# A four-block graph network on one core: a comparison of edge types goes to GpSimd, four bias rows are loaded at two places, and the last output tile is added and stored in halves

## The chip, the core and the metric

The kernel runs on one core of a Trainium2 chip. The core has five engines that run their own queues of instructions and wait for each other by semaphores: TensorE (PE, matrix products into PSUM), VectorE (DVE), ScalarE (ACT), GpSimd (POOL) and SyncE (SP), which here only issues transfers. Transfers between the chip's memory (HBM) and the on-chip SBUF are issued from SP, from GpSimd and, twice at the start, from ScalarE, and are carried out by 16 DMA engines. The metric is device microseconds of one execution; lower is better.

## The reference

A graph has 1024 nodes with 512 features each (x) and 17408 edges (src, dst, sorted by dst), the loops among them. Each edge has 4 attributes for block 1, 8 for its small network, a type of 8 and a weight. Four blocks follow each other, each of the form x + block(relu(layernorm(x))):

```
block 0: adj (deduplicated, symmetric, with loops), scaled by 1/sqrt(degree) on both sides; adj @ (h @ W) + bias
block 1: w = network(edge attributes 8) -> 4 x 128 per edge; messages w * up(h)[src] * edge attributes 4;
         sums by dst; a linear map out
block 2: twice  h @ W0 + (norm-weighted sum of h over edges) @ W1 + b;  between them
         layernorm * gamma + beta and a leaky relu   (rows b1, gamma, beta, b2 of 512)
block 3: twice  h @ loop + bias + sum over 4 bases of (sums by dst of coef * h[src]) @ basis,
         coef = comp[type of the edge] * weight of the edge; a relu between them
```

The output is x after block 3, 1024x512 in float32.

## The kernel before, in words

Nodes lie in 8 tiles of 128. Edges lie in 136 tiles of 128, taken two at a time as 68 groups. Because edges are sorted by destination, the two tiles of a group fall in a window of 32 nodes; the kernel checks that at run time and has a general path for other graphs (`stack(False)`), which isn't taken here.

*Counting (about 30 to 97 us).* A matrix `cnt` of 1024x1024 counts the edges between nodes. For each group VectorE has made one-hot rows by comparing a ramp with the edge's source (`ro`, 128x1024) and its destination in the window (`co`, 128x2048), for eight edge tiles at a time (`places`, L504); TensorE multiplies them into PSUM (`pc`, L532), and VectorE adds the product into the window of `cnt` (L545). Between these, TensorE does the rest of block 0's dense layer (`pz`, L251) and the first 13 of 17 batches of the edge network (`hidden`: `pm` on TensorE, L453, an activation on ScalarE, L455, and a write of the third layer to the table `hidtab` in HBM, L458, from SP for batches 0, 3, 6 and 9 and from GpSimd for the others). TensorE's order in this stage is fixed as written. The load of the edge types (`relations`, L434, 64 rows of 2176) is issued from SP behind the write of batch 6; `related` (L440) compares them with the row's own number and is written in the code at group 59 of 68 (`if g == NG * 7 // 8`). Its result feeds 34 small products (`related_bases`, `pr`, L594), which come after the products `pa` (L618, L620) that turn the finished counts into adjacency.

*Block 1 (about 165 to 476 us).* Per group, TensorE makes the edge weights (`pw`, L819) from a batch of `hidtab` rows that SP has fetched (`fetch`, L576; two buffers, a new batch every four groups, listed in `fetched`); GpSimd gathers the source rows of two tiles (L290) and weights the window (`yo`, L859); ScalarE and VectorE make the messages (L836 to L841); TensorE sums them (`pg`, L885) and VectorE adds the sums (L888). Among these, block 2's weights are loaded, and GpSimd subtracts blocks of them (`sums_of_blocks`, L765).

*Block 2 (about 476 to 690 us).* The rows b1, gamma, beta and b2 are spread to 128 partitions by four loads from SP (`bias_row`, L104; four buffers in rotation, shared with the bias of block 0 and those of block 3). b1 is added at L986, gamma and beta used at L1008 and L1009, and b2 added at L1011. The code stands behind block 1's, but the four loads are tied behind one fetch:

```
with tc.issue_after(fetched[8]):
    b1 = bias_row("L2_gnn_b1", f"b1{fast}")
    gamma = bias_row("L2_gnn_gamma", f"gamma{fast}")
    beta = bias_row("L2_gnn_beta", f"beta{fast}")
    b2 = bias_row("L2_gnn_b2", f"b2{fast}")
```

*Block 3 (about 690 to 1219 us).* Twice over 68 groups: gathers (L290), a weighted window (`wo`, L1135), sums `ps` (L1149) and their addition (L1168). As soon as a node tile has all its edges, its products with the four bases follow (`products`, `po`, 16 per tile, L1094); `ready` adds the result, and in the second layer stores the tile (L1086, L1087). The last tiles' products stand at the end.

*What sets the order.* A planner goes over the traced instructions and puts each in the queue of its engine, using its own estimate of when its inputs are there; instructions further down in the code may come earlier in a queue. `tc.issue_after(ins)` keeps what is traced under it, on the engine of `ins`, behind `ins`. `pinned` keeps the instructions of the named engines in the order in which they are written. Otherwise only data and buffers hold an instruction back.

Of the kernel before, what the change touches and what calls it, by code (L numbers as in the profile page):

```python
# [15 lines left out]
ALU = mybir.AluOpType  # L16
# [5 lines left out]
P = 128  # L22
N = 1024
NB = N // P
D = 512
KC = D // P
# [5 lines left out]
NREL = 8  # L32
NBAS = 4
# [16 lines left out]
def gnn_stack(ctx, tc, a, out, xtab, htabs, hidtab):  # L50
# [6 lines left out]
    nc = tc.nc  # L57
# [25 lines left out]
    x = const.tile([P, NB, D], F32, name="x")  # L83
# [74 lines left out]
    r8 = const.tile([P, 1], F32, name="r8")  # L158
# [120 lines left out]
    def split(terms, n, z, scale, name, rest=None):  # L279

        hi, mid, lo = (t[:, n, :] for t in terms)
        nc.scalar.activation(hi, z, AF.Copy, scale=scale)
        if rest is None:
            rest = work.tile([P, D], F32, tag="h", name=f"rest_{name}", bufs=4)
        nc.vector.scalar_tensor_tensor(rest, z, scale, hi, op0=ALU.mult, op1=ALU.subtract)
        nc.scalar.copy(mid, rest)
        return nc.vector.tensor_sub(lo, rest, mid).ins
# [59 lines left out]
    with pinned(PE):  # L347
# [7 lines left out]
        for _ in first:  # L355
# [8 lines left out]
                                            op0=ALU.add, op1=ALU.subtract))  # L364
# [22 lines left out]
    def stack(fast):  # L387
# [43 lines left out]
        def relations(pool):  # L431

            types = pool.tile([8 * NREL, E // 8], I32, name="types")
            nc.sync.dma_start(types, bass.AP(tensor=a["edge_type_8"].tensor, offset=0, ap=[[E // 8, 8], [0, 8], [1, E // 8]]))  # L434
            return types

        def related(types):

            rel = types.bitcast(F32)
            nc.vector.tensor_scalar(rel, types, r8[: 8 * NREL], None, op0=ALU.is_equal)  # L440
            return rel


# [33 lines left out]
        with tc.tile_pool(name=f"ohs{fast}", bufs=6 if fast else 4) as ohs, pinned(PE):  # L477
            if fast:
# [44 lines left out]
                for g in range(NG):  # L523
# [11 lines left out]
                    if behind and behind[0] in written:  # L535

                        with tc.issue_after(written[behind[0]]):
                            if behind.pop(0) == 6:
                                types = relations(rels)
                            else:  # L540
                                next(loads)
                    if g == NG * 7 // 8:
                        rel = related(types)
                    part = cnt[:, :, bass.ds(base(g), W)]
                    nc.vector.tensor_add(part, part, pc.rearrange("p (i w) -> p i w", w=W))  # L545
            else:
# [6 lines left out]
                for g in range(ET // B):  # L553
# [3 lines left out]
                    for i in range(NB):  # L557
                        for j in range(2):
                            ps = bank(f"pc_{g}_{i}_{j}")
                            for k in range(B):  # L560
                                nc.tensor.matmul(ps, so[k][:, i * P : (i + 1) * P], do[k][:, j * 512 : (j + 1) * 512],
                                                 start=(k == 0), stop=(k == B - 1))
# [9 lines left out]
        hq, fetched = {}, []  # L572
# [38 lines left out]
        if fast:  # L611

            degs = small.tile([P, 2, NB], F32, tag="degs", name="degs", bufs=1)
            for i in range(NB):
                for j in range(2):
# [3 lines left out]
                    for q in range(4):  # L619
                        nc.tensor.matmul(pt[:, q * P : (q + 1) * P], cnt[:, 4 * j + q, i * P : (i + 1) * P], ident16,  # L620
                                         start=False, stop=(q == 3))
# [36 lines left out]
        for n in range(NB):  # L658
            if fast:
                last = split(terms, n, zs0[:, n, :], dinv[:, n : n + 1], f"0_{n}")  # L660
# [148 lines left out]
        with tc.tile_pool(name=f"l1e{fast}", bufs=2 if fast else 1, reuse_waits="tile") as l1e:  # L809
# [43 lines left out]
            if fast:  # L853
# [16 lines left out]
                for g in range(NG):  # L870
# [11 lines left out]
                    for i in range(len(prods[0])):  # L882
                        for k in range(G):
                            lhsT, rhs, b, n = prods[k][i]
# [32 lines left out]
        with tc.tile_pool(name=f"l2{fast}", bufs=1) as l2:  # L917
# [3 lines left out]
            else:  # L921
                terms1 = [l2.tile([P, NB, D], F32, tag="parts1", name="zs2")]
            y = stage
            with tc.issue_after(fetched[8]):
                b1 = bias_row("L2_gnn_b1", f"b1{fast}")
                gamma = bias_row("L2_gnn_gamma", f"gamma{fast}")
                beta = bias_row("L2_gnn_beta", f"beta{fast}")
                b2 = bias_row("L2_gnn_b2", f"b2{fast}")

# [98 lines left out]
            def bases(l):  # L1028

                ws = [load_w(a[f"L3_gnn_basis{l}"][b], f"basis{l}_{b}{fast}") for b in range(2)]  # L1030
                return ws + [[load_half(w_l0[h], a[f"L3_gnn_basis{l}"][2], h) for h in range(2)]]

            loops = {0: loop_weights(0)}
            w3 = [loops[0][0]] + bases(0)
# [30 lines left out]
        with tc.tile_pool(name=f"l3{fast}", bufs=1, reuse_waits="tile") as l3:  # L1065

            sums = l3.tile([P, KC, NBAS, N], F32, name="sums")
# [9 lines left out]
            def ready(l, n, po):  # L1077

                if l == 0:
                    nc.vector.tensor_add(hb[:, n, :], hb[:, n, :], po)  # L1080
                    nc.scalar.activation(hb[:, n, :], hb[:, n, :], AF.Relu)  # L1081
                    nc.sync.dma_start(htabs[1][n * P : (n + 1) * P, :], hb[:, n, :])
                    if fast:
                        nc.gpsimd.memset(sums.rearrange("p c b d -> p (c b) d")[:, :, n * P : (n + 1) * P], 0.0)
                else:
                    nc.vector.tensor_add(x[:, n, :], x[:, n, :], po)  # L1086
                    nc.sync.dma_start(out[n * P : (n + 1) * P, :], x[:, n, :])  # L1087

            def products(l, n, w3):

                po = bank2(f"po3_{l}_{n}")[:, 0, :]
                for b in range(NBAS):
                    for c in range(KC):
                        nc.tensor.matmul(po, sums[:, c, b, n * P : (n + 1) * P], chunk(w3[1 + b], c),  # L1094
                                         start=(b == 0 and c == 0), stop=(b == NBAS - 1 and c == KC - 1))
                        if b == NBAS - 1 and c == KC - 1:
                            ready(l, n, po)
                        yield

            for l in range(2):  # L1100
                if l == 1:
                    w3 = [loops[1][0]] + bases(l)
# [3 lines left out]
                with tc.tile_pool(name=f"l3e{l}{fast}", bufs=3 if fast else 1, reuse_waits="tile") as l3e:  # L1106
# [24 lines left out]
                    if fast:  # L1131
# [10 lines left out]
                        for g in range(NG):  # L1142
# [8 lines left out]
                            n = {0: 3, 1: 4, 2: 5, 4: 6, 6: 7}.get(g)  # L1151
# [19 lines left out]
                    else:  # L1171
                        for g in range(NG):
                            m = gathered(g)
                            for b in range(NBAS):
                                for j in range(2):
# [5 lines left out]
                                    for c in range(KC):  # L1181
                                        ps = bank(f"ps_{l}_{g}_{b}_{j}_{c}")
                                        for k in range(G):
                                            nc.tensor.matmul(ps, m[k][:, c * P : (c + 1) * P], wo[:, k, :],
                                                             start=(k == 0), stop=(k == G - 1))
# [75 lines left out]
```

## Time and profile before

| | us |
|---|---|
| median of three runs | 1225.16 |
| the three runs | 1224.23, 1227.38, 1225.16 |
| the profiled execution | 1221.29 |
| its span, first to last instruction | 1219.5 |
| TensorE busy in it | 1195.6 |
| VectorE busy | 661.8 |
| GpSimd busy | 580.5 |
| ScalarE busy | 295.0 |

The profile is of one execution. Its rows give an engine, a line of the kernel, what is written from what, shapes and counts; times in brackets are idle time of that engine just ahead, with what ended it. The chain that ended last is followed back from the last instruction: at each step to what released it, or to the one before it on its engine. PEld is TensorE's loading of weights, which runs beside its products. A name with q (DVEq, SPq) is an engine's own queue, where register work, waits and issues are done. "issue" is time in which an engine waited for nothing that the profile shows. The clock granted to TensorE was 0.994 of full speed over the span.

### The profile page before, as it was taken

Reading aid. Unit: us, or ns where it says so; the run is one execution under the profiler, and the core shown is the slowest. Engines: PE = TensorE matmul, PEld = TensorE weight load, DVE = VectorE, ACT = ScalarE, POOL = GpSimd, SP = SyncE. Lnnn points to the kernel's source line nnn. Section 1 sums busy time; section 2 is a strip of 40 time slices with the busy share of each in tenths; the row PEclk is TensorE's granted clock in tenths of the full one; section 3 lists DMA queues with packets and bytes.
Section 4 is the critical chain, followed back from the end, with each engine's and each line's share of the span. In section 5 each row is a group of like instructions: output and inputs, shape, how many; then the busy total and the mean of one; then the engine's idle time right before and its main releaser. Section 6 shows DMA issues by size and latency. Waiting matters only on the chain.

```text
span 1219.5 us, 17420 instructions
## 1 busy us (share of the span) xinstructions
PE 1195.6 (98%) x6322; PEld 795.8 (65%) x6322; DVE 661.8 (54%) x1244; ACT 295.0 (24%) x693; POOL 580.5 (48%) x641
## 2 busy tenths in 40 slices
PE   7999999999999999999999999999999999999998
PEld 3445557767777778644444567777776577777774
DVE  5888647786777775776774433333332153333331
ACT  4435364434444443432332400000000000000000
POOL 2011346686666663443121266566661586555540
PEclk9999999989999999999999999999999999999999
DMA  3331045545544442002002366555552666556540
GB/s 114 124 125 36 22 155 165 151 139 153 151 139 139 139 130 85 21 22 65 1 9 92 101 193 206 160 164 157 165 163 65 199 170 194 162 162 170 157 129 17
DMA packets 55166, 149.77 MB, mean 123 GB/s; under 512 B 8796, under 2 KB 10272, under 8 KB 55008
## 3 DMA queue, kind: packets, MB, share of 16 engines
q0 software_dynamic: 33360, 109.34, 31.3%
q1 hardware_dynamic: 21424, 38.71, 9.6%
q8 instruction: 52, 0.85, 0.3%
q10 hardware_dynamic: 288, 0.52, 0.1%
q14 instruction: 42, 0.34, 0.1%
HBM read 135.70 MB, written 12.85 MB: 122 GB/s over the span
## 4 chain that ended last, share of the span: by engine, by line
PE 89%; DVE 4%; issue 2%; DMA 2%; ACT 1%; POOL 1%; DVEq 0%; SPq 0%; ACTq 0%; POOLq 0%
PE ps L1149 19%; PE po L1094 18%; PE pg L885 14%; PE pu L275 10%; PE pw L819 10%; PE p L955 7%; PE pl L251 4%; PE pm L453 2%; PE po L803 1%; PE pz L251 1%; PE pt_l L241 1%; PE pc L532 1%; DVE cnt L545 1%; PE pup L689 1%; DMA w_mlp<-in_L_gnn_W_mlp_dram 1%
## 5 line engine op out<-in xcount | busy, mean ns | idle before, releaser
L290 POOL DMA_INDIRECT m<-htab_dram,src_i x272 | 261.2, 960 | 165.6 <-PE ps L1149 116.9
L1149 PEld LDWEIGHTS ps<-wo,m 128*128 128x128 f32 x2176 | 261.6, 192 | 57.3 <-issue 56.0
L1149 PE MATMUL ps<-wo,m 128*128 128x128 f32 x2176 | 262.2, 275 | 0.7 <-DMA m<-htab_dram,src_i 0.7
L885 PEld LDWEIGHTS pg<-yo,msg 128*128 128x128 f32 x1632 | 194.6, 193 | 35.9 <-issue 17.8
L885 PE MATMUL pg<-yo,msg 128*128 128x32 f32 (+1 forms) x1632 | 189.8, 274 | 2.7 <-DVE msg L841 1.5
L1168 DVE TENSOR_TENSOR sums<-sums,ps 128x512 f32 x136 | 93.7, 689 | 156.7 <-PE po L1094 133.8
L836 ACT ACTIVATE dot<-s,ea 128x128 f32<-128x128 f32 x408 | 130.0, 390 | 165.7 <-DVE msg L841 107.5
L290 POOL DMA_INDIRECT s<-xtab_dram,src_i x136 | 132.8, 976 | 36.4 <-issue 24.5
L819 PE MATMUL pw<-w_mlp,hq 128*128 128x512 f32 x272 | 135.1, 620 | 0.0
L1135 DVE TENSOR_TENSOR wo<-ohw,cwTrue 128x256 f32<-128x256 f16 x136 | 65.9, 487 | 103.5 <-PE ps L1149 103.5
L859 POOL TENSOR_TENSOR yo<-ohw,ea 128x160 f32<-128x160 f16 x136 | 63.1, 486 | 66.6 <-PE pg L885 66.5
L275 PE MATMUL pu<-parts,cnt 128*128 128x512 bf16 x384 | 84.8, 379 | 0.0
L837 DVE TENSOR_TENSOR msg<-pw,s 128x512 f32<-128x512 f32 x68 | 47.0, 692 | 47.3 <-PE pw L819 35.6
L819 PEld LDWEIGHTS pw<-w_mlp,hq 128*128 128x128 f32 x272 | 47.2, 193 | 34.0 <-issue 34.0
L275 PEld LDWEIGHTS <-cnt 128*128 128x128 f16 x384 | 37.6, 98 | 44.9 <-issue 2.3
L838 DVE TENSOR_TENSOR msg<-s,pw 128x768 f32<-128x768 f32 x68 | 64.2, 944 | 0.0
L1094 PE MATMUL po<-basis_0True,sums 128*128 128x512 f32 x128 | 60.8, 600 | 0.4
L1094 PE MATMUL po<-basis_3True,sums 128*128 128x512 f32 x128 | 59.8, 594 | 0.8 <-DVE sums L1168 0.8
L1081 ACT ACTIVATE stage<-stage 128x512 f32<-128x512 f32 x8 | 5.0, 630 | 226.9 <-DVE stage L1080 226.9
L1094 PE MATMUL po<-w_l,sums 128*128 128x512 f32 x128 | 59.9, 593 | 0.0
L1094 PE MATMUL po<-basis_1True,sums 128*128 128x512 f32 x128 | 59.9, 593 | 0.0
L888 DVE TENSOR_TENSOR acc<-acc,pg 128x256 f32 x68 | 28.7, 422 | 46.7 <-PE pg L885 46.7
(208 smaller groups left out, 1355.2 us busy)
## 6 DMA issues: line engine op xcount, KB each, us to landing
hq<-hidtab_dram SPq DMA_DIRECT2D x17, 256.0 KB, 2.9
m<-htab_dram,src_i POOLq DMA_INDIRECT x272, 3.6
hidtab_dram<-hid POOLq DMA_DIRECT2D x9, 256.0 KB, 2.3
s<-xtab_dram,src_i POOLq DMA_INDIRECT x136, 3.6
xtab_dram<-up SPq DMA_DIRECT2D x8, 256.0 KB, 2.0
b_1True<-in_L_gnn_W_dram SPq DMA_DIRECT2D x4, 512.0 KB, 5.0
w_l<-in_L_gnn_basis_dram SPq DMA_DIRECT2D x4, 512.0 KB, 4.3
basis_0True<-in_L_gnn_basis_dram SPq DMA_DIRECT2D x4, 512.0 KB, 4.0
```

The source lines that it names most:

```text
L275: nc.tensor.matmul(pu, m[:, s, d * P : (d + 1) * P], z[:, s, :], start=(s == 0 and j == 0), stop=(s == NB - 1 and j == len(zs) - 1))
L290: nc.gpsimd.indirect_dma_start(out=g, out_offset=None, in_=table, in_offset=bass.IndirectOffsetOnAxis(ap=idx[:, t : t + 1], axis=0))
L819: nc.tensor.matmul(pw[:, k, :], hq[q][:, (t % 4) * P : (t % 4 + 1) * P], w_mlp4[:, t // 4 % 2, :], start=True, stop=True)
L836: nc.scalar.activation(dot[:, k, m, :], s1[:, k, m, :], AF.Copy, scale=ea[:, g * G + k, 1 + m : 2 + m])
L838: nc.vector.tensor_mul(msg[:, :, 2:5, :], s1, w[:, :, 2:3, :].to_broadcast([P, G, 3, MUL]))
L859: nc.gpsimd.tensor_mul(yo[:, k], ohw[:, t, :].unsqueeze(1).to_broadcast([P, NY, W]), ea[:, t, :].unsqueeze(2).to_broadcast([P, NY, W]))
L885: nc.tensor.matmul(ps[:, b : b + n, :], lhsT, rhs, start=(k == 0), stop=(k == G - 1))
L955: nc.tensor.matmul(p, lhs[:, c, :], rhs[:, c, :], start=(c == 0), stop=(c == 1))
L1094: nc.tensor.matmul(po, sums[:, c, b, n * P : (n + 1) * P], chunk(w3[1 + b], c), start=(b == 0 and c == 0), stop=(b == NBAS - 1 and c == KC ...
L1135: nc.vector.tensor_mul(wo, ohw[:, ts, :].unsqueeze(2).to_broadcast([P, G, NBAS, W]), cw[:, l, ts, :].unsqueeze(3).to_broadcast([P, G, NBAS ...
L1149: nc.tensor.matmul(ps[:, c * P : (c + 1) * P], m[k][:, c * P : (c + 1) * P], wo[:, k].rearrange("p b w -> p (b w)"), start=(k == 0), stop= ...
L1168: nc.vector.tensor_add(part, part, ps.rearrange("p (i w) -> p i w", w=W))
```

## The change

Three edits. `related` runs on GpSimd in place of VectorE, with the same operands. The rows b1 and gamma are tied behind `fetched[9]`, and beta and b2 behind `fetched[12]`. In the second layer of block 3, node tile 7 is added and stored in two halves of 256 columns; the other tiles are as before. (A local name `last` in `products` only shortens its text.)

```
-            nc.vector.tensor_scalar(rel, types, r8[: 8 * NREL], None, op0=ALU.is_equal)
+            nc.gpsimd.tensor_scalar(rel, types, r8[: 8 * NREL], None, op0=ALU.is_equal)
...
-            with tc.issue_after(fetched[8]):
+            with tc.issue_after(fetched[9]):
                 b1 = bias_row("L2_gnn_b1", f"b1{fast}")
                 gamma = bias_row("L2_gnn_gamma", f"gamma{fast}")
+            with tc.issue_after(fetched[12]):
                 beta = bias_row("L2_gnn_beta", f"beta{fast}")
                 b2 = bias_row("L2_gnn_b2", f"b2{fast}")
...
-                    nc.vector.tensor_add(x[:, n, :], x[:, n, :], po)
-                    nc.sync.dma_start(out[n * P : (n + 1) * P, :], x[:, n, :])
+                    for h in (slice(0, D // 2), slice(D // 2, D)) if n == NB - 1 else (slice(0, D),):
+                        nc.vector.tensor_add(x[:, n, h], x[:, n, h], po[:, h])
+                        nc.sync.dma_start(out[n * P : (n + 1) * P, h], x[:, n, h])
```

More of the change, by code (lines that the diff above doesn't have):

```diff
@@ L1093, in products @@
                     for c in range(KC):
-                        nc.tensor.matmul(po, sums[:, c, b, n * P : (n + 1) * P], chunk(w3[1 + b], c),
-                                         start=(b == 0 and c == 0), stop=(b == NBAS - 1 and c == KC - 1))
-                        if b == NBAS - 1 and c == KC - 1:
+                        last = b == NBAS - 1 and c == KC - 1
+                        nc.tensor.matmul(po, sums[:, c, b, n * P : (n + 1) * P], chunk(w3[1 + b], c), start=(b == 0 and c == 0), stop=last)
+                        if last:
                             ready(l, n, po)
```

## The prediction

> **What bounds the kernel now.** I read the page first (busy shares), then the chain that ended last, once for the whole span and once around each of the three places that the change touches, and then the instructions there in order of time. The page's shares:
>
> ```profile
> PE 1195.6 (98%) x6322; PEld 795.8 (65%) x6322; DVE 661.8 (54%) x1244; ACT 295.0 (24%) x693; POOL 580.5 (48%) x641
> PE 89%; DVE 4%; issue 2%; DMA 2%; ACT 1%; POOL 1%; DVEq 0%; SPq 0%; ACTq 0%; POOLq 0%
> ```
>
> TensorE is 98% busy and carries 89% of the chain, so an edit elsewhere pays only where the chain leaves TensorE. Does it at the three places? First the counting: the chain between 74 and 92 us.
>
> ```profile
> 74.61 0.43 DVE cnt L545
> 75.08 0.39 PE pc L532 x2
> 75.47 0.86 PE pm L453 x2
> ...
> 78.86 0.42 DVE cnt L545
> 79.32 0.39 PE pc L532 x2
> ...
> 81.69 0.61 ACT hid L455
> ...
> 87.00 0.99 PE pz L251 x2
> 87.99 0.23 PE pc L532 x2
> 88.22 0.86 PE pz L251 x2
> ```
>
> Up to about 80 us the chain keeps passing through VectorE (the count's additions, and behind "issue" its one-hot comparisons); from 81 us it is TensorE and ScalarE alone. Now VectorE itself around the comparison that moves:
>
> ```profile
> 87.84 1.34 DVE L440 TENSOR_SCALAR types<-types,r 64x2176 f32<-64x2176 int32 x1
> 89.11 0.41 DVE L545 TENSOR_TENSOR cnt<-cnt,pc 128x256 f32 x1
> ...
> 94.75 0.42 DVE L545 TENSOR_TENSOR cnt<-cnt,pc 128x256 f32 x1 [0.28 <-PE pc L532]
> 95.83 0.42 DVE L545 TENSOR_TENSOR cnt<-cnt,pc 128x256 f32 x1 [0.67 <-PE pc L532]
> ```
>
> The comparison takes 1.34 us at a time when the chain is elsewhere, and the last additions wait for TensorE (0.28 and 0.67 us): VectorE has caught up. Second, the chain where the four bias rows are issued (300.1 to 302.0 us):
>
> ```profile
> 299.72 2.60 PE pg L885 x24
> 302.32 1.80 PE pw L819 x4
> 304.12 2.60 PE pg L885 x24
> 306.71 1.80 PE pw L819 x4
> 308.51 2.60 PE pg L885 x24
> ```
>
> It is TensorE without a gap, one group each 4.40 us. Third, the end, in order of time:
>
> ```profile
> 1215.65 0.69 DVE L1086 TENSOR_TENSOR x<-x,po 128x512 f32<-128x512 f32 x1 [13.04 <-PE po L1094]
> 1216.37 0.33 SPq L1087 DMA_DIRECT2D out_dram<-x  x1
> ```
>
> Here all is exposed: one addition, one store, and the span's end at 1219.5 us.
>
> **The base.** The profiled execution took 1221.29 us for its span of 1219.5, 1.79 us lying around it. It is 3.87 us below the median of the three runs shown (1225.16; 1224.23 to 1227.38). I sum differences on the profiled execution and add them to the median.
>
> **Edit 1, the types compared by GpSimd.** Removed: 1.34 us of VectorE at 87.84. What it hid behind is TensorE's row of eight pz steps and nine pc pairs up to 96.65, with waits only for ScalarE's copies (0.45 and 0.67 us). Worth: 0. If that cover were gone, 1.34 us at most. Late next is TensorE itself.
>
> Added: one instruction of 64x2176 with one tensor input on GpSimd. The trace has none like it, so I bound its duration D by GpSimd's rows. The memset of 128x4096 took 3.51 us, 0.86 ns an element: D = 1.9 us. The additions of 128x512 with two inputs took 1.28 us alone, 2.5 ns an element: D = 5.4 us. The 128x128 multiplication at L141 has the instruction's own operation, took 0.73 us, and taken whole (5.7 ns an element) gives 12.4 us. But the VectorE comparison co started inside that multiplication (77.62 against 77.38) and took 1.31 us instead of 1.22, so it was held up 0.09 us, not 0.49. I take it that most of the 0.73 us was waiting, and D is nearest to the one-input memset: 2.2 us, with 1.9 and 5.4 as ends and 12.4 as the far one.
>
> When does it run? The planner puts ready GpSimd work early: the block subtractions of L765 stand in the code at groups 28 to 56 and ran from 249 to 265 us, around groups 16 to 19. So I expect the comparison not at group 59 but as soon as the types land. Their load was issued at 64.66, no landing is shown; loads of 512 KB took 4 to 6 us, so about 70 us. That is where the chain still runs over VectorE. What a GpSimd operation can do to VectorE is shown by these rows, in order of time:
>
> ```profile
> 252.84 1.28 POOL L765 TENSOR_TENSOR t_1True<-b_1True 128x512 f32<-128x512 f32 x1
> 252.91 5.98 DVE L839 TENSOR_TENSOR dot<-dot 128x256 f32<-128x256 f32 x1
> ...
> 254.06 2.50 POOL L765 TENSOR_TENSOR b_1True<-b_1True 128x512 f32<-128x512 f32 x2
> ```
>
> An addition of two SBUF tensors that takes 0.42 us elsewhere started 0.07 us after GpSimd and took 5.98 us, as long as GpSimd ran without a pause. The reverse also stands in the trace: one GpSimd addition at L667 took 5.71 instead of 1.26 us beside the 4.74 us comparison at L672. The count's additions read one operand from PSUM; the comparisons ro (0.69 us) and co (1.22 us) read two from SBUF. They come once in four groups, 1.8 of some 3.9 us; a GpSimd operation that ends within the other 2.1 us costs nothing. A start right after co (70.84 us) leaves ro at 72.88 as the next that can be held: it loses D - 2.0, 0.2 us. A start just ahead of ro loses all of D, 2.2 us. If ro or co runs first, GpSimd waits for them and is in the first case. Averaged over the moment at which the types land: 1.8/3.9 x 0.2, and 2.1/3.9 x 1.2 (the mean of 0.1 and 2.2), together +0.7 us. The ends are 0 and +5.4; a gain is excluded but for the 1.34 above.
>
> The Trainium skill, page "SBUF — State Buffer", section "Who interferes with whom", says that the pair of ports shared by the two engines is an exclusive lock, that a VectorE instruction with two SBUF inputs contends with a GpSimd one that reads SBUF, and that the second to start is blocked until the first ends. The 5.98 us row agrees, and goes further, as several GpSimd instructions were waited out. By the rule alone a GpSimd start ahead of ro costs all of D, +2.2 in place of +0.7.
>
> Queued behind the new instruction on GpSimd are the remaining writes of hidden rows (71.83, 79.66, 81.50, 86.20). If it waits for the types at 70 us and runs 2.2, the write of 71.83 goes about 0.5 us later; six hidden buffers are in rotation and the fetch of those rows comes in the next stage, so 0. Placed two writes earlier, the write of 65.88 would wait some 6.5 us and ScalarE's next use of that buffer with it: up to 4 us, a mishap of the same sign that I keep in the range. After 86.2 the next GpSimd work is at 117.46. The 34 products pr that read the result start at 104.48, so the result may be over 15 us late.
>
> **Edit 2, the bias rows.** Each is one issue on SP of 0.38 to 0.43 us and 256 KB, landing after 4.8 to 6.6 us. Two move from 300.1 behind the fetch at 317.34, two behind the one three further (each 17.6 us apart, so 370). Nothing else on SP stands between the fetches, and a fetch is issued a group ahead of its use. The buffers are free (the last user of the fourth, the first bias, ended at 131.9). First use is at 484.31 (b2) and 507.39 (b1), over 110 us later. The waits for gathers at 303 to 309 (up to 2.14 us) are ScalarE's, and TensorE goes on at 4.40 us. So: 0 removed, 0 added. With cover gone the bound is a row's landing, 6.6 us; a gain is excluded, as the chain there has no gap to close.
>
> **Edit 3, the last tile in halves.** Now: addition 0.69, issue at 1216.37, end at 1219.5. After: two additions of 128x256, each 0.42 us by L545, the second starting 0.33 after the first (such additions start at 260.27, 260.61 and 260.94), so the second ends at 1216.39, +0.05. SP issues the first store at about 1216.12; issues in a row stand 0.48 apart (300.12, 300.60, 301.07), so the second is at 1216.60, +0.23. It moves 128 KB in place of 256; between 1217 and 1218 the engines were 70% busy at 262 GB/s, so the whole took about 0.9 us and half saves 0.44. Net -0.2 us. Ends: -0.4 (no delay in issue) and +0.5 (nothing saved, an issue of 0.48 added).
>
> The Trainium skill, page "DMA: Bandwidth & Descriptors", section "Anatomy of one DMA", gives some 2.0 us fixed for each DMA (told there of those that GpSimd issues), mostly the receipt of the last byte, which halving doesn't shorten; it speaks against two stores. The trace has 2.0 us from issue to landing for 256 KB (the shortest of eight), no more than that; by the page alone nothing is saved and edit 3 is +0.2.
>
> **Sum.** 0 + 0.7 + 0 - 0.2 = +0.5 us: 1221.8 for the profiled execution, 1225.7 on the median.
>
> **The rivals.**
> *GpSimd holds VectorE for long* (slower). Place: 70 to 80 us, where the chain runs over cnt L545. For: the 5.98 us row, and L141's duration taken whole. Against: co was held only 0.09 us beside L141, and the write of 71.83 keeps GpSimd from an early block. D = 5.4 gives up to +5.2 in all, 1230.4; D = 12.4, less 2.0 of free time, gives +10.2, 1235.4. It decides by more than 3.7 us from D = 5.9 upward with a start after co, or 3.9 just ahead of ro.
> *The planner orders later work differently* (faster). The message groups' products began at 249.61, 253.84, 259.64 and 268.94; at 4.40 us each the last was due at 262.8. It was 6.1 us late, for two held additions (5.98 and 3.13 us). Another order could undo that, 1225.7 - 6.1 = 1219.6, or add as much again, 1231.8. For: GpSimd's queue is planned and an instruction is added to it. Against: the added one is 150 us earlier, the moved rows 40 us later, and neither is on that queue at that place.
> *The comparison does not move early*: it runs behind the write of 86.20, VectorE gains 1.34 us that nobody waits for, total -0.2, 1225.0.
>
> **How the numbers follow.** Forecast 0.36 and its near relative, the late comparison, 0.25; held for long 0.27, of which 0.23 beyond 3.7 us; planner 0.12, 0.08 of it faster, 0.04 slower. A difference under 0.3% (3.7 us) is about what a measurement of this kernel can tell from no change. Faster 0.08; slower 0.23 + 0.04 = 0.27; within 0.65. The likeliest's own range is 1223.5 to 1228.5 (the runs' spread of 1 to 2 us about the median, and the ends of edit 3). For 8 in 10 I leave out the faster case (0.08) and the longest D (about 0.1): 1222 (the forecast less the runs' spread and edit 3's gain) to 1232 (D = 5.4 in full with the runs' spread).
>
> **What would show it.** Right: a GpSimd row at L440 of 1.9 to 2.7 us near 70 us; ro or co near it longer by under 1 us; first pa product within 1 us of 96.49; pg still at 4.40 us from 300 to 380; two stores at the end and the span ending within 0.5 us after its last addition as now. Wrong: L440 over 5 us on GpSimd with a long ro or co inside it; hidden activations waiting for a write; or groups in the message stage in another order, which would show as a changed start of pg after 265 us.

## The result, and the profile after

| | before | after |
|---|---|---|
| median, 22 runs each (us) | 1223.65 | 1226.46 |
| lowest and highest (us) | 1218.97, 1227.38 | 1221.65, 1231.62 |
| the profiled execution, its span (us) | 1221.29, 1219.5 | 1228.83, 1227.0 |

The ratio after to before is 1.0030, 95% interval 1.0018 to 1.0043: 3.7 us slower, 2.2 to 5.3 (the means of the 22 runs lie 3.7 us apart, the medians 2.8). The time lies in the predicted range (1222 to 1232) and 0.8 us from the forecast of 1225.7. But the forecast's own difference was +0.5 us, so it is the difference that has to be explained. The two profiled executions lie 7.5 us apart, further than the medians; the runs of the kernel before fall into two groups, near 1220 and near 1226 us, and its profile is from the lower one.

The page's shares and the chain's hardly moved:

```profile
PE 1197.2 (98%) x6306; PEld 797.0 (65%) x6322; DVE 666.4 (54%) x1244; ACT 295.0 (24%) x693; POOL 587.6 (48%) x642
PE 90%; DVE 4%; issue 2%; DMA 2%; ACT 1%; POOL 1%; DVEq 0%; SPq 0%; ACTq 0%; POOLq 0%
```

GpSimd is busy 7.1 us more, VectorE 4.6 us more although the comparison has left it, TensorE 1.6 us more for the same products. Nothing here says where. The first product `pa` behind the counting does: it began at 96.49 us before, at 103.85 after, and from it to the span's end it is 1123.0 us before and 1123.15 after. All of the difference in these two executions arises ahead of it (1.3 us of the 7.4 was there at GpSimd's first write of hidden rows, 45.79 against 44.48 us, ahead of any edit). So the view to read is the counting, in order of time. GpSimd first, then VectorE, then TensorE:

```profile
67.17 0.54 POOL L458 DMA_DIRECT2D hidtab_dram<-hid  x1 [6.72 <-ACT hid L455]
73.44 5.80 POOL L440 TENSOR_SCALAR types<-types,r 64x2176 f32<-64x2176 int32 x1 [5.73 <-DMA types<-in_edge_type_dram]
79.21 0.62 POOL L458 DMA_DIRECT2D hidtab_dram<-hid  x1
```

```profile
70.14 0.68 DVE L504 TENSOR_TENSOR ro<-ramp,row 128x1024 f16<-128x1024 f16 x1
...
73.91 5.77 DVE L504 TENSOR_TENSOR ro<-ramp,row 128x1024 f16<-128x1024 f16 x1
79.61 1.30 DVE L504 TENSOR_TENSOR co<-ramp,col 128x2048 f16<-128x2048 f16 x1
```

```profile
81.29 0.59 PE L532 MATMUL pc<-co,ro 128*128 128x256 f16 x2 [5.30 <-DVE cnt L545]
81.68 1.91 PE L453 MATMUL pm<-hid,w_mlp 128*128 128x512 f32 x2
...
85.95 1.02 PE L453 MATMUL pm<-hid,w_mlp 128*128 128x512 f32 x2
```

The comparison stands between two writes of hidden rows and took 5.80 us. It began 0.47 us ahead of a `ro`, and that `ro` took 5.77 us instead of 0.68, to 0.4 us past the comparison's end. TensorE then stood 5.30 us, named as a wait for the count. When it starts again its products are slower: 1.91 us for a pair that takes 1.02 four microseconds later. The stretches show why (us, then busy time of TensorE, its weight loads, VectorE, ScalarE and GpSimd, then the granted clock, DMA share and GB/s):

```profile
76.00:78.00 2.00, 0.00 (x0) 0.00 (x0) 2.00 (x1) 0.60 (x1) 2.00 (x1) 1.00 0.97 271
78.00:80.00 2.00, 0.00 (x0) 0.10 (x1) 2.00 (x2) 0.00 (x0) 1.97 (x3) 0.66 1.00 301
80.00:82.00 2.00, 0.71 (x3) 0.64 (x3) 1.66 (x3) 0.00 (x0) 1.30 (x1) 0.50 0.77 276
82.00:84.00 2.00, 2.00 (x5) 0.61 (x5) 1.54 (x4) 0.38 (x1) 0.00 (x0) 0.50 0.07 27
84.00:86.00 2.00, 2.00 (x8) 0.96 (x6) 1.80 (x3) 0.30 (x2) 0.00 (x0) 0.63 0.00 0
86.00:88.00 2.00, 2.00 (x8) 0.83 (x8) 1.77 (x4) 1.11 (x2) 0.10 (x1) 1.00 0.00 0
```

While TensorE idles its clock falls, to 0.50 by 80 us, and it is full again from 86. The work lost to it is 0.71 x 0.50 + 2 x 0.50 + 2 x 0.37 = 2.1 us. The wait and the clock together are 7.4 us, of which some replaces waits that were there before (TensorE was idle 0.7 us between 72 and 80 in the kernel before, too). So the counting is 6.1 us longer in this pair (7.4 less 1.3), while all runs together differ by 3.7; the record has no profile of the kernel before from its upper group, and why the runs differ by less than this pair isn't shown.

The other two places. The bias rows, on SP, and the chain at the time of the first two:

```profile
325.42 0.42 SPq L104 DMA_DIRECT2D row_b1True<-in_L_gnn_b_dram  x1
325.89 0.42 SPq L104 DMA_DIRECT2D row_gammaTrue<-in_L_gnn_gamma_dram  x1
...
378.18 0.43 SPq L104 DMA_DIRECT2D row_betaTrue<-in_L_gnn_beta_dram  x1
```

```profile
320.62 2.60 PE pg L885 x24
323.22 1.80 PE pw L819 x4
325.01 2.60 PE pg L885 x24
327.61 1.80 PE pw L819 x4
```

One group still takes 4.40 us, with no gap. And the end: the last addition is now

```profile
1223.34 0.75 DVE L1088 TENSOR_TENSOR x<-x,po 128x256 f32<-128x256 f32 x2 [13.05 <-PE po L1097]
```

From its start to the span's end it is 3.66 us, where it was 3.85 before.

### The profile page after: what moved, and what is told of

Its sections match the earlier page's. It is cut to its first block, busy times and chain, and to the rows that moved or that the text cites. A ratio compares the mean times of both kernels' runs of the same rounds, so it can differ in the third digit from the quotient of the medians.

```text
span 1227.0 us, 17411 instructions
## 1 busy us (share of the span) xinstructions
PE 1197.2 (98%) x6306; PEld 797.0 (65%) x6322; DVE 666.4 (54%) x1244; ACT 295.0 (24%) x693; POOL 587.6 (48%) x642
## 4 chain that ended last, share of the span: by engine, by line
PE 90%; DVE 4%; issue 2%; DMA 2%; ACT 1%; POOL 1%; DVEq 0%; SPq 0%; ACTq 0%; POOLq 0%
PE ps L1151 19%; PE po L1097 18%; PE pg L885 14%; PE pu L275 10%; PE pw L819 10%; PE p L956 7%; PE pl L251 4%; PE pm L453 3%; PE po L803 1%; PE pz L251 1%; PE pt_l L241 1%; PE pc L532 1%; PE pup L689 1%; DMA w_mlp<-in_L_gnn_W_mlp_dram 1%; DVE cnt L545 1%
```

## The experiments

Each ratio is against the kernel before, run beside it on the same chip. The chips differ (medians of the kernel before: 1232.8 and 1236.2 us in the first two sets, 1222.6 and 1222.2 in the later ones), so only ratios are compared between sets, and from profiles of different sets only what single instructions and waits take. Diffs are against the kernel before, except where said. A small difference that shows in the profile can be lost in the median over the runs, so for the causes I read both.

**1. Which edit costs the time?** Edit 1 alone:

```
-            nc.vector.tensor_scalar(rel, types, r8[: 8 * NREL], None, op0=ALU.is_equal)
+            nc.gpsimd.tensor_scalar(rel, types, r8[: 8 * NREL], None, op0=ALU.is_equal)
```

> Edit 1 alone (types compared by GpSimd; rows and last tile as before). Theory A, GpSimd locks VectorE out: the whole loss is here, 3 to 7 us over the kernel before; the comparison takes 5.8 us near 73 us, one ro takes about as long instead of 0.68, TensorE idles some 5 us and its granted clock falls to half for some 6 us; first adjacency product pa at about 103 us, against 96.5. Theory B, the moved rows or the halved store cost it: no loss here, within 1 us of before.

Edits 2 and 3 alone:

```
-            with tc.issue_after(fetched[8]):
+            with tc.issue_after(fetched[9]):
...
+            with tc.issue_after(fetched[12]):
...
+                    for h in (slice(0, D // 2), slice(D // 2, D)) if n == NB - 1 else (slice(0, D),):
+                        nc.vector.tensor_add(x[:, n, h], x[:, n, h], po[:, h])
+                        nc.sync.dma_start(out[n * P : (n + 1) * P, h], x[:, n, h])
```

> Edits 2 and 3 without edit 1 (types compared by VectorE). Theory A: -0.2 us against before, not to be told from no change; pg at 4.40 us throughout 300 to 400 us; time from the last addition's start to the end of the span 3.66 us, against 3.85 before. Theory B: 3 to 4 us slower, with a gap in pg where the rows land (318 or 370 us).

All three, with GpSimd's comparison held back behind the last `co` by a small copy that reads it (diff against the changed kernel):

```
-                    if g == NG * 7 // 8:
-                        rel = related(types)
+                    if g == NG * 7 // 8 + 1:
+                        late = small.tile([P, 8], F32, tag="late", name="late", bufs=1)
+                        with tc.issue_after(nc.gpsimd.tensor_copy(late, nxt[1][:, 0, :8, 0]).ins):
+                            rel = related(types)
```

> All three edits, but the comparison on GpSimd is held until the last co is written (about 91 us), by a small copy of it on GpSimd. Theory A: the comparison still takes 1.9 to 5.8 us, but VectorE has only additions with a PSUM operand then; no ro or co is long, TensorE doesn't idle, pa starts within 1 us of 96.5, and the kernel is within 1 us of before. If a comparison on GpSimd were costly in any place (theory C: slower hand-over to the products pr, or code loading on GpSimd), the loss would stay at 3 us or more, or pr would start later than 8 us after the first pa.

Measured, 12 runs each. Edit 1 alone: 1.0028 (1.0008 to 1.0049). Edits 2 and 3: 1.0015 (0.9994 to 1.0035), not told apart from no change; its profile has 176.00 us of TensorE in the 176 between 300 and 476 us. All three with the comparison late: 0.9995 (0.9976 to 1.0014). The loss is edit 1's, and it goes when the same instruction runs elsewhere. It is no shorter there:

```profile
90.33 1.22 DVE L504 TENSOR_TENSOR co<-ramp,col 128x2048 f16<-128x2048 f16 x1
91.47 0.94 DVE L547 TENSOR_TENSOR cnt<-cnt,pc 128x256 f32 x2
91.62 0.19 POOL L544 CAST late<-co 128x8 f32<-128x8 f16 x1 [3.77 <-DVE co L504]
91.80 5.79 POOL L440 TENSOR_SCALAR types<-types,r 64x2176 f32<-64x2176 int32 x1
```

5.79 us, but with no `ro` or `co` left that could meet it; the additions with an operand in PSUM beside it keep their 0.42 us. The first `pa` starts at 97.61 us, 1.1 later than before, of which 0.9 was there at GpSimd's first write (45.42 us). Theory A, a lock, stands; B (the other edits) has no support, and C (the comparison costs wherever it runs) falls.

**2. What makes the comparison 5.8 us?** Four probes on GpSimd at 139 to 159 us, on the buffer of the types, which is free by then. They were added to the changed kernel, though the expectation speaks of the kernel before:

```
+                    probe = nc.gpsimd.tensor_scalar(rel, rel, r8[: 8 * NREL], None, op0=ALU.is_equal).ins
...
+                    probe = nc.gpsimd.tensor_scalar(rel, rel.bitcast(I32), r8[: 8 * NREL], None, op0=ALU.is_equal).ins
...
+                    probe = nc.gpsimd.tensor_scalar(rel, rel, 2.0, None, op0=ALU.mult).ins
...
+                    nc.gpsimd.tensor_copy(rel, rel.bitcast(I32))
```

> The kernel before, with four instructions more on GpSimd between 130 and 160 us, each on the comparison's own 64x2176 buffer, whose values are no longer used by then: the comparison with f32 read, with int32 read, a multiplication by a fixed number in f32, and a copy from int32 to f32. H (the 5.80 us come from the int32 reading): the f32 comparison takes 1.9 to 3 us and the int32 one 5.8. I (GpSimd takes 2.67 ns for each element in any one-input arithmetic): comparison 5.8 for both types, multiplication about the same, copy about the same. J (the comparison, or its operand that is a column of the tile, is the dear part): both comparisons 5.8, multiplication and copy under 3. VectorE's additions of two SBUF tiles beside them are held for as long as each runs.

The groups of that stretch (busy us, mean ns of one):

```profile
L670 POOL TENSOR_SCALAR types<-types,r 64x2176 f32<-64x2176 f32 x1 | 5.8, 5797 | 0.0
L672 POOL TENSOR_SCALAR types<-types,r 64x2176 f32<-64x2176 int32 x1 | 5.8, 5776 | 0.1
L674 POOL TENSOR_SCALAR types<-types 64x2176 f32<-64x2176 f32 x1 | 5.7, 5720 | 0.1
L676 POOL CAST types<-types 64x2176 f32<-64x2176 int32 x1 | 2.0, 1992 | 0.1
```

Neither the integers nor the comparison: arithmetic with one input takes 2.6 to 2.7 ns a column on GpSimd, a copy 0.92. The last clause of that expectation was not tested, because VectorE had no addition of two SBUF tiles there: its reductions and its operations with an operand in PSUM ran beside these probes at their own durations (1.21 and 0.74 us), as they do without them. Theory I holds for arithmetic, not for the copy.

**3. Does the loss follow the length?** Only half, or a quarter, of the columns on GpSimd early, the rest on VectorE at group 59 (diff against the changed kernel; 32 in place of 16 for the quarter):

```
-            nc.gpsimd.tensor_scalar(rel, types, r8[: 8 * NREL], None, op0=ALU.is_equal)
+            half = E // 16
+            nc.gpsimd.tensor_scalar(rel[:, :half], types[:, :half], r8[: 8 * NREL], None, op0=ALU.is_equal)
+            nc.vector.tensor_scalar(rel[:, half:], types[:, half:], r8[: 8 * NREL], None, op0=ALU.is_equal)
```

> All three parts of the change, but GpSimd compares only the first half of the columns early; the other half stays on VectorE at group 59 (0.67 us there, half of 1.34). A (the comparison locks VectorE out for as long as it runs, and the clock falls when TensorE idles over some microseconds): GpSimd's comparison takes 2.9 us (half of 5.80), ro beside it 2.5 us instead of 5.8, TensorE's wait for the count after it about 2.4 us instead of 5.3 to 5.5, and the granted clock stays near 1.00 between 78 and 86 us, where the changed kernel had 0.50; the loss is under half of the changed kernel's, 0 to 1.5 us of its 3.4. F (the loss comes from the comparison's wait for the types, 5.73 us, which stands in GpSimd's queue ahead of a write of the hidden rows): the wait is the same with half the columns, so the loss is the same, 2.8 us or more, and ratio 1.002 to 1.003. G (a fixed cost of GpSimd's first comparison): 4 us or more for half the columns, and a loss near the whole.

> As the half, with a quarter of the columns on GpSimd (1.45 us by A) and three quarters on VectorE at group 59 (1.0 us). A: ro 1.2 us instead of 5.8, the wait of TensorE behind it under 1.3 us, clock 1.00, and a time within 0.1% of the kernel before. F: the same loss as the changed kernel, 2.8 us or more. G: 4 us or more for the quarter too.

Half: 0.9995 (0.9967 to 1.0023); quarter: 0.9984 (0.9957 to 1.0011). GpSimd took 3.05 and 1.66 us, the wait for the types in front of it was the same as before (5.83 and 5.73 us), and the clock stayed at 1.00. So G falls, and F, taken as the whole cause, does too. But A had a miss of its own, in GpSimd's and VectorE's rows of the half:

```profile
73.58 3.05 POOL L441 TENSOR_SCALAR types<-types,r 64x1088 f32<-64x1088 int32 x1 [5.83 <-DMA types<-in_edge_type_dram]
```

```profile
73.97 1.31 DVE L506 TENSOR_TENSOR ro<-ramp,row 128x1024 f16<-128x1024 f16 x1
75.21 1.21 DVE L506 TENSOR_TENSOR co<-ramp,col 128x2048 f16<-128x2048 f16 x1
```

`ro` was to be held 2.5 us, to GpSimd's end at 76.63. It was out at 75.28, and `co` ran at its own length with GpSimd still at work. The lock is not held to the end. In the quarter `ro` took 0.68 us, where A expected 1.2.

**4. How long is it held?** Comparisons of several widths on GpSimd, on 64 rows beside the types, each meant to start ahead of a `ro`, by way of a small copy of `co` and a filler of 544 columns:

```
+                tried = {3: [E // 8], 6: [E // 16], 9: [E // 32] * 4, 12: [3 * E // 32], 15: [E // 16] * 2}
...
+                        for width in [E // 32] + tried[j]:
+                            with tc.issue_after(behind_co):
+                                behind_co = nc.gpsimd.tensor_scalar(tries[:, :width].bitcast(F32), tries[:, :width], r8[8 * NREL :], None, op0=ALU.is_equal).ins
```

> The kernel before, with comparisons of different widths tried on GpSimd during the counting, on 64 rows of their own beside the types: behind the 3rd, 6th, 9th, 12th and 15th column comparison (co) of VectorE comes a filler of 544 columns, and then one of 2176 columns, one of 1088, four of 544, one of 1632, and two of 1088, so placed that the next ro falls under them. L (a GpSimd comparison holds VectorE's two-operand comparisons to its end only when it is long; a short one lets them in after 0.6 us or at once, as with 1088 and 544 columns before): ro under 2176 takes 4 us or more, under 1088 1.3 us or less, under four of 544 and under two of 1088 no more than 1.5 us, and 1632 shows where the limit lies. M (any GpSimd comparison may hold or let in, by the moment at which the two meet): no order by width; ro beside 2176 may be as short as 0.7 us, and beside a short one as long as the short one is. N (the hold is as long as GpSimd has work without a break): four of 544 and two of 1088 hold ro for 4 us or more, as 2176 does.

VectorE's comparisons beside 2176 columns, beside 1088 (`co` and the next `ro`), 544 and 1632, in this order; then GpSimd's instruction of 1088:

```profile
40.65 4.94 DVE L508 TENSOR_TENSOR ro<-ramp,row 128x1024 f16<-128x1024 f16 x1
...
57.48 1.22 DVE L508 TENSOR_TENSOR co<-ramp,col 128x2048 f16<-128x2048 f16 x1
...
60.64 0.68 DVE L508 TENSOR_TENSOR ro<-ramp,row 128x1024 f16<-128x1024 f16 x1
...
76.37 0.92 DVE L508 TENSOR_TENSOR ro<-ramp,row 128x1024 f16<-128x1024 f16 x1
...
81.28 3.57 DVE L508 TENSOR_TENSOR ro<-ramp,row 128x1024 f16<-128x1024 f16 x1
```

```profile
57.12 4.40 POOL L520 TENSOR_SCALAR types<-types,r 64x1088 f32<-64x1088 int32 x1
```

With the half above and the changed kernel, the time from GpSimd's start to the moment at which `ro` can have started (its end less 0.68 us) is:

| columns | GpSimd (us) | held from GpSimd's start (us) |
|---|---|---|
| 2176 (changed kernel; this run) | 5.80; 5.79 | 5.56; 5.4 |
| 1632 | 4.39 | 3.2 |
| 1088 (the half) | 3.05 | 1.0 |
| 544 (at 76.03 us here) | 1.64 | 0.6 |

L holds in these meetings: at most 1.0 us of hold up to 1088 columns, nearly all of the instruction at 2176, 1632 between; 1632 and 1088 have one meeting with a `ro` each. The order by width speaks against M. N falls by the four of 544, beside which `ro` took 0.83 and 0.92 us; the two of 1088 met no `ro`. And the lock works both ways: the 1088 of this run began 0.36 us ahead of a `co`, which ran at its own length, and took 4.40 us itself instead of 3.04. Why the hold grows faster than the length, no run here shows.

**5. So cut it into pieces?** The changed kernel with four pieces:

```
+            for i in range(4):
+                part = slice(i * E // 32, (i + 1) * E // 32)
+                nc.gpsimd.tensor_scalar(rel[:, part], types[:, part], r8[: 8 * NREL], None, op0=ALU.is_equal)
```

> The changed kernel, with the comparison on GpSimd made in four instructions of 544 columns instead of one of 2176, in the same early place: the same 5.8 to 6.6 us of GpSimd's time. L: ro and co keep 0.7 to 1.5 us, TensorE's wait for the count behind them is under 1.5 us, the granted clock stays at 1.00 between 74 and 88 us, and the 3 us of the changed kernel are gone: ratio 0.998 to 1.0005. N: ro takes 5 us or more as in the changed kernel, and the ratio is 1.002 to 1.003.

A miss in the time, though right in its mechanism: 1.0034 (1.0012 to 1.0056). `ro` took 0.68 and `co` 1.66 and 1.22 us, so VectorE was let in. A new wait took the old one's place. GpSimd, then ScalarE, then TensorE:

```profile
72.08 7.95 POOL L442 TENSOR_SCALAR types<-types,r 64x544 f32<-64x544 int32 x4 [6.22 <-DMA types<-in_edge_type_dram]
79.98 0.60 POOL L460 DMA_DIRECT2D hidtab_dram<-hid  x1
```

```profile
82.43 1.08 ACT L457 ACTIVATE hid<-pm 128x512 f32<-128x512 f32 x2 [4.30 <-DMA hidtab_dram<-hid]
```

```profile
83.08 1.56 PE L455 MATMUL pm<-feats,w_mlp 128*128 128x512 f32 x2 [2.69 <-ACT hid L457]
```

Now GpSimd is the one that waits (7.95 us, where four pieces alone take 6.6, 4 x 1.64), and behind it in its queue stands the write of the ninth block of hidden rows, issued at 71.83 us in the kernel before. Its buffer stays taken, ScalarE waits 4.30 us for it, TensorE 2.69, and the clock is 0.91 and 0.50 in the two stretches from 82 to 86 us.

**6. That write on SP's queue.** To the pieces, and to the changed kernel as it is:

```
-                    written[q] = (nc.sync if q in (0, 3, 6, 9) else engine).dma_start(hidtab[q * P : (q + 1) * P, :], f).ins
+                    written[q] = (nc.sync if q in (0, 3, 6, 8, 9) else engine).dma_start(hidtab[q * P : (q + 1) * P, :], f).ins
```

> The comparison in four pieces of 544 columns on GpSimd, and the write of the ninth block of hidden rows, which stood behind them in GpSimd's queue until 79.98 us, on SP's queue instead. F2 (in pieces the loss comes from that write: the buffer of the hidden rows stays taken, the activation after it waits 4.3 us for the write's landing, TensorE 2.7 us for the activation, and the clock falls to 0.50): the activation's wait is under 1.5 us, TensorE's wait for hid under 1 us, the clock 1.00 from 74 to 90 us, and the ratio is 0.998 to 1.0008. Rival (the pieces cost VectorE, or something that these two windows do not show): the loss of the pieces stays, ratio 1.002 to 1.004.

> The changed kernel with the comparison whole, and the same write on SP's queue. A (the hold of ro alone makes the loss): ro takes 5 us or more, TensorE waits 5 us for the count, the clock falls to 0.50, ratio 1.0018 to 1.004 as in the changed kernel. F (the write behind the comparison makes it): ro is long, yet the time is that of the kernel before, ratio under 1.001. Both take part: between them.

Pieces: 0.9983 (0.9964 to 1.0002), median 1220.43 us. Whole: 1.0028 (1.0010 to 1.0045), median 1226.60. The pieces' waits and clock (the waits of TensorE between 70 and 105 us are total, times, longest):

```profile
PE pm L455 <- ACT hid L457: 1.1, 3, 0.5
...
PE pc L534 <- DVE cnt L547: 0.4, 1, 0.4
```

```profile
82.00:84.00 2.00, 1.42 (x5) 0.57 (x5) 1.69 (x4) 0.66 (x2) 2.00 (x3) 1.00 0.00 0
84.00:86.00 2.00, 1.94 (x10) 1.15 (x11) 1.88 (x3) 0.84 (x2) 0.03 (x2) 1.00 0.71 262
```

The whole comparison, with the write moved, still has its long `ro` and TensorE's wait for the count:

```profile
71.77 5.48 DVE L504 TENSOR_TENSOR ro<-ramp,row 128x1024 f16<-128x1024 f16 x1
```

```profile
78.86 0.39 PE L532 MATMUL pc<-co,ro 128*128 128x256 f16 x2 [5.02 <-DVE cnt L545]
```

Its clock is 0.50 from 80 to 82 us. So the hold alone makes the changed kernel's loss, and the write behind the comparison makes the pieces'. Between the two kernels with the write moved, which differ only in the cutting, lie 6.2 us of the medians and 4.4 of the spans. The pieces with the write moved are not shown to beat the kernel before: the interval reaches past 1.

**7. The same lock elsewhere.** The additions of 5.98 and 3.13 us that the prediction read at 253 us are still there after (6.02 and 3.13). Can they be had back? First GpSimd's eight subtractions tied behind the gathers of every fourth group, so that they don't stand in a row:

```
+                    drawn.append(gather(s[:, k, :], xtab, src_i, g * G + k).ins)
...
-                        with tc.issue_after(fetched[-1]):
+                        with tc.issue_after(fetched[-1]), tc.issue_after(drawn[-1]):
```

> The kernel before with one thing changed: GpSimd's block subtractions in the message stage are tied behind the gathers of groups 28, 32 ... 56, in place of running together at 249 to 265 us. The same lock at another place: if GpSimd work without a pause holds VectorE's additions of two SBUF tensors (5.98 and 3.13 us there) and so costs the 6.1 us by which the groups fell behind, this is 5 to 6 us faster than before, with no L839 over 2 us and pg at 4.40 us from 200 to 470 us. If those long rows cost nothing, it is the same as before.

A miss: 0.9996 (0.9976 to 1.0015). Between 240 and 300 us TensorE is now busy without a gap at full clock, but a single subtraction still goes with a long addition (VectorE, then GpSimd):

```profile
310.52 2.52 DVE L839 TENSOR_TENSOR dot<-dot 128x256 f32<-128x256 f32 x1
310.65 1.29 POOL L765 TENSOR_TENSOR t_1True<-b_1True 128x512 f32<-128x512 f32 x1
311.87 0.88 POOL L859 TENSOR_TENSOR yo<-ohw,ea 128x160 f32<-128x160 f16 x2
```

Seven of the eight did so (2.51 to 2.70 us instead of 0.42). This addition began 0.13 us ahead of the subtraction and came out at 313.04 us, 0.3 us behind the two weightings that follow the subtraction without a pause. So here an addition was held until GpSimd paused, as in the row of 5.98 us, whereas the short comparisons of run 4 let VectorE in between. The operations and types differ, and no run here shows which of them matters.

Between 300 and 476 us TensorE was idle 2.4 us of 176, and its clock was 0.83 in two stretches of 10 us (from 330 and from 370), which is 3.3 us of lost work. In the kernel before it was idle 2.4 us between 240 and 300, and the lowered clock of 260 to 270 (0.70, then 0.62) lost it 3.1. The gain was moved, not made. In that profile there is also a wait of 5.5 us near 1013 us, ahead of a tile's products with the bases. Waits of 2.3 to 5.5 us stand at the same products in four profiles of runs 1 and 3, so it is not this edit's; its cause I did not find. With the subtractions on VectorE, in the same spread places:

```
-                    nc.gpsimd.tensor_tensor(o[:, c, :], p[:, c, :], q[:, c, :], op=ALU.subtract)
+                    (nc.vector if halves == 2 else nc.gpsimd).tensor_tensor(o[:, c, :], p[:, c, :], q[:, c, :], op=ALU.subtract)
```

> The kernel before, with the eight subtractions of the first block (128x512, f32) put from GpSimd to VectorE, one behind the gathers of each fourth group, instead of eight in a row on GpSimd at 249 to 265 us. A: no GpSimd instruction over 1 us is left beside VectorE's additions, so the long additions (5.98 and 3.13 us) are gone, TensorE has no idle stretch and clock 1.00 between 249 and 280 us; VectorE pays eight times about 0.75 to 0.95 us (its addition of 128x256 takes 0.45) out of its idle 28% there, which hides them; 4 to 6 us faster, ratio 0.995 to 0.997. K (VectorE has no room in the group in which the subtraction falls): each delays the group's products by about its length, so what is gained at 250 to 270 us is lost again, 0 to 2 us faster.

The largest miss: 1.0106 (1.0069 to 1.0144). Each takes 0.685 us, no addition is long, and each makes TensorE wait about 0.5 us for the messages (3.6 us in seven waits), as K said. With these waits alone it would still be some 2 us to the good (6.1, the lateness that the prediction read, less 3.6); what turns it in the profile is the clock:

```profile
380.00:390.00 10.00, 9.49 (x62) 7.50 (x62) 6.18 (x12) 3.84 (x12) 6.31 (x9) 0.99 0.53 147
390.00:400.00 10.00, 10.00 (x32) 7.33 (x32) 4.83 (x10) 3.72 (x12) 3.54 (x6) 0.50 0.28 77
400.00:410.00 10.00, 10.00 (x31) 6.98 (x30) 3.24 (x6) 1.86 (x6) 2.81 (x4) 0.50 0.18 52
```

For 20 us TensorE is busy at half clock, half the products in each stretch, 10 us lost; four more stretches of 10 us between 330 and 450 us have 0.83 to 0.95. It is not the profiled run's alone: the mean clock of all ten runs is 0.974 to 0.986, that of the kernel before beside them 0.986 to 0.994. The only idle time ahead of it is 0.51 us. What brought the clock down there stays open.

## Why the prediction was right or wrong

*The time, the range, the class.* 1226.46 us lies in the range. The step that gives the difference, +0.5 us, was too small; measured are 3.7 (2.2 to 5.3). The forecast's time was near by luck, because its base was the median of three runs, 1225.16, where 22 runs gave 1223.65. The ratio sits on the bound of 0.3% that divided "within" from "slower".

*"The comparison moves early, as soon as the types land, about 70 us."* Right: it was queued behind the write of 67.17 us and waited 5.73 us for the types, until 73.44. Their load, issued at 65.95, took 7.5 us where 4 to 6 were expected. The rival in which it does not move early is out.

*"D is nearest to the one-input memset: 2.2 us, with 1.9 and 5.4 as ends."* This is the step that failed. The term that it feeds, +0.7, was too small for it. D is 5.80, outside its near ends. The runs price GpSimd's one-input arithmetic at 2.6 to 2.7 ns a column, as dear as its two-input addition; only the copy (0.92) is near the memset (0.86). The prediction had the row of the right operation, L141, and explained its 0.73 us away as waiting, because `co` beside it was hardly held. In a quiet place (the run of widths) L141 took 0.54 us, so at most 0.2 of it was waiting. That `co` was hardly held beside it fits the short instructions of run 4, which held VectorE little or not at all though they worked throughout; it was no sign that GpSimd was waiting.

*"Averaged over the moment at which the types land, +0.7."* The mean stood for a spread of outcomes, and the kernel has one: the start fell just ahead of a `ro`, by 0.36 to 0.64 us in the four profiles that have the whole comparison early (the changed kernel, edit 1 alone, the probes, and the write moved). For that case the prediction said that all of D is lost. With D = 5.8 that is 5.2 to 5.8 us, and TensorE's wait was 5.0 to 5.3 in the four. The mechanism and its place (the rival "GpSimd holds VectorE for long", given 0.27) were right.

*Left out: the clock.* A stall of 5.3 us is followed by 2.1 us lost at half clock, which no term held. The trace of before had the pattern: 2.4 us of idling between 255 and 265 us, and the clock at 0.70 and 0.62 in the two stretches of 5 us from 260 to 270. The Trainium skill, page "TensorE: Matmul & The Clock Gate", Part 1, puts the array at half clock after an idle window of some 3.4 us; here the clock fell within 5.30 us of idling, which agrees, but in the pieces it fell after a wait of 2.69 us, which is shorter. The 0.51 us of the last experiment is not what that rule would lead one to expect.

*The lock.* The prediction took it as exclusive until the first instruction ends, and the Trainium skill, page "SBUF — State Buffer", section "SBUF: two separate sides", says the same, for the whole instruction. For 2176 columns the row agrees (held 5.56 of 5.80 us); for 1088 it doesn't (1.0 of 3.05), nor for 544 (0.6 of 1.64). The measurement decides: for this comparison the length matters more than in proportion.

*"It waits for the types, so the write of 71.83 goes 0.5 us later... So 0."* The write went at 79.21, 7.4 us later (1.3 of it that profile's own lateness). In the changed kernel it cost nothing that shows, because TensorE and so the activations stood still meanwhile: with the write on SP the loss stayed (1.0028). With VectorE let in, it cost the whole loss again (1.0034 against 0.9983). The mishap was named in the prediction, for another write; its "up to 4 us" is near the 4.30 us that ScalarE waited.

*Edit 1's removal, worth 0.* With the comparison out of everybody's way on GpSimd the ratio is 0.9995 (0.9976 to 1.0014): no gain that shows, as said.

*Edit 2, worth 0.* Shown: 4.40 us a group, before and after, and 176.00 us of 176 in the run of edits 2 and 3.

*Edit 3, -0.2 us.* The tail from the last addition's start is 3.85 before and 3.66 after, -0.19; the halves land in 1.7 and 1.8 us where the whole took 2.0, so the halving saved 0.2 to 0.3 us there and not 0.44, and the sum came out right partly by luck. The +0.2 that the prediction set against it, "by the page alone", left out that the page's cost has a second part that grows with the bytes. All this is read from the profiles; no median here can tell 0.2 us.

*"The planner orders later work differently."* It did not: the pair of long additions is as before (6.02 and 3.13 us), and so is the order in the message stage.

## What to carry to other kernels

An instruction moved to GpSimd "because it is idle" costs twice: its own time, here 4.3 times that of VectorE (5.80 against 1.34 us), and the time for which VectorE's operations on two SBUF operands can't start. Look for what VectorE does at the moment at which the planner will really place it, and for what stands behind it in GpSimd's queue, transfers above all; cutting it into short pieces let VectorE in here, but the time came back only when the write behind them was moved away as well. Price an operation by the row of that operation, however small, before a row of a cheaper kind, and where a stall of some microseconds is expected, add what the lowered clock costs behind it (2.1 us behind 5.30 here).

## What was not expected of the hardware

- GpSimd: one-input arithmetic of 64x2176 takes 5.7 to 5.8 us with the two types and two operators tried, a copy of it 1.99. By width it is 1.64, 3.04, 4.39 and 5.79 us for 544, 1088, 1632 and 2176 columns.
- The hold on VectorE is not proportional to that: 0.6, 1.0, 3.2 and 5.4 us. Pieces back to back let VectorE in between and are held themselves (7.95 us for four, 8.88 in the run with the write moved, where they take 6.6 alone).
- TensorE's clock can stand at 0.50 for 20 us while it is busy throughout, 0.51 us of idling ahead of it (the last profile of run 7). No run here explains it.
